# Deformable convolution network on Trainium2: variances from a moving operand, and an earlier first statistic with half of the rows kept

## The chip, the cores and the metric

The kernel runs on one NeuronCore of a Trainium2 chip (trn2). A core has five engines that work side by side, each with its own instruction queue: TensorE (PE in the profile; its weight loads are listed apart as PEld), VectorE (DVE), ScalarE (ACT), GpSimd (POOL) and SyncE (SP), and 16 DMA engines that move data between HBM and the on-chip memories SBUF and PSUM. The metric is the device time of the whole program in microseconds (us), as the median of several runs.

## The reference

The input is x, 8 images of 64 channels, 128x128 pixels, float32. Four layers follow one another, each of the form x = x + layer(groupnorm(x)):

```python
x = x + _L0_conv_ref(_gn(x), ...)   # deformable 3x3 convolution
x = x + _L1_conv_ref(_gn(x), ...)   # 3x3 convolution
x = x + _L2_conv_ref(_gn(x), ...)   # two state-space (S5) blocks, along rows and along columns
x = x + _L3_conv_ref(_gn(x), ...)   # nearest neighbours in a window, and upsampling
```

`_gn` is a group norm over pairs of channels, so every layer needs sums over all pixels of an image before its first output. Layer 0 computes, for every pixel and each of nine taps, an offset (a 1x15 plus a 15x1 convolution, `wh` and `wv`) and a mask (a 3x3 convolution, `wm`), samples the normed image bilinearly at the shifted point, and applies the 64x64x3x3 weights `wd`. It then has a batch norm over all images. Layer 2 begins with a layer norm over the 64 channels of a pixel, `(x - mu) * rsqrt(var + 1e-5) * g + b`; its result feeds a linear recurrence along the pixels, forward and backward.

## The kernel before

**Layout.** Two images make a pair: 64 channels of each fill the 128 partitions, and the 16,384 pixels lie along the free dimension. There are four pairs. Pixels are handled in chunks of 512, 32 a pair. Each engine's instruction order is fixed when the program is built, by a scheduler that follows the order of the program text, the free buffers of each pool, and the data that is ready. A pool tag with one buffer (`bufs=1`) makes the next writer wait for the last reader of that tag.

**Start, pair 0.** `deform` first prepares constants: it issues the zero rows and columns of the four gather tables on ACT's queue (L203 and the two lines after), loads the offset weights and biases on SP's queue (L211 to L232), and copies the weights into `wt` on DVE and POOL (28 of these copies are DVE's, L218). Then:

- `statistics` (L262) loads x in eight pieces of 128x2048 (L267, tag "xs", two buffers), takes `bn_stats` of each quarter (L269), and `groupnorm` turns these into the scale and shift of the norm.
- `fill` (L274) loads x again in eight pieces (L287), norms each on ACT (L288), transposes it on PE (L291), copies it from PSUM into `q`, and writes it pixel by pixel into the gather table in HBM.
- `offsets` (L305) loads a strip `xe` of up to 22 rows (L311), norms it on ACT (L312), runs the offset convolutions on PE with the weights `wt` (L323), evicts on ACT into `ob` (L333), transposes, and computes indices and bilinear weights on DVE (with a sigmoid on ACT, L379).

**Gather stage.** `sample` then issues 9216 indirect DMAs on POOL (L405), each of which fetches four corners of 128 pixels; DVE weights and adds them (L414, L415), PE transposes and multiplies by `wd`. Between them `work` advances two lists of other work by small steps: `near`, the offsets of the next strip, and `far`, the setup of the later layers' constants (`setup_scan` and others, for pair 0), then statistics and fill of the next pair.

**After the gathers**, for each pair: `finish_deform`, `conv3x3` (with the previous pair's nearest-neighbour layer beside it), and `scan_layer`. The latter runs `first_norm` together with the backward scan of the first direction, then the forward scan, then the second direction.

**First norm.** It goes through eight groups (n = 7 to 0) of four chunks. For each chunk PE multiplies by a centring matrix (L887, PSUM tag "x", two buffers), ACT writes the square into `sq` (L889, tags "sq" and "xt" in turn, one buffer each) and the centred values into `bf` (L890), and `variances` (L847) sums the squares over channels on PE:

```python
for q in range(4):
    at = first + 2 * q
    self.nc.tensor.matmul(pv[:, at : at + 2], lhsT=sq[:, q * P : (q + 1) * P], rhs=self.imgmean, start=True, stop=True)
```

Here a quarter of the squares is the stationary operand and the 128x2 matrix `imgmean` (1/64 for the channels of one image) the moving one; the result has pixels on partitions. After four chunks `rsqrt` (L105) computes 1/sqrt(var + eps) on DVE, beginning with the addition of eps (L109). One group later `scale` widens these roots on POOL (`spread`, L857), transposes them back on PE (L860, tag "y", two banks), and multiplies the centred values on DVE (L879). After each group the backward scan makes two steps: `inputs` on ACT (L1205) and four DMAs that rearrange, `drive` (PE L1216 and L1219, a copy to `v` on ACT L1218, two multiplications on DVE, an addition on POOL L1223), and `scan` (PE L1231, ACT L1236, DVE L1238).

Of the kernel before, what the change touches and what calls it, by code (L numbers as in the profile page):

```python
# [9 lines left out]
F32 = mybir.dt.float32  # L10
# [6 lines left out]
P = 128  # L17
C = 64
# [23 lines left out]
class Net:  # L42
# [33 lines left out]
    def setup_constants(self):  # L76
        nc, const = self.nc, self.const
        with self.tc.tile_pool(name="setup", bufs=1) as sp:
# [21 lines left out]
            self.imgmean = const.tile([P, 2], F32, name="imgmean")  # L100
            nc.vector.tensor_copy(self.imgmean, mean.rearrange("p (a b) -> p a b", b=C)[:, :, 0])
# [3 lines left out]
    def rsqrt(self, pool, v, n, eps, tag):  # L105
# [3 lines left out]
        nc.vector.tensor_scalar_add(ve, v, eps)  # L109
# [67 lines left out]
    def deform(self):  # L177
# [6 lines left out]
        with ExitStack() as ctx:  # L184
# [11 lines left out]
            with tc.tile_pool(name="a_setup", bufs=1) as sp:  # L196
                zeros = sp.tile([P, 2 * PW], F32, name="zeros")
                nc.gpsimd.memset(zeros, 0.0)
                for table in (t for pair in tables for t in pair):
                    flat = table.rearrange("a b q -> a (b q)")  # L200
                    n = LINE * PW // P
                    for row in (0, CELL - 1):
                        nc.scalar.dma_start(flat[row : row + 1, :].rearrange("a (p n) -> (a p) n", p=P), zeros[:, 0:n])  # L203
                    for r0, r1 in ((1, CELL - 1 - 1), (CELL - 2, CELL - 1)):
                        nc.scalar.dma_start(flat[r0:r1, 0 : 2 * PW], zeros[0 : r1 - r0, :])
                        nc.scalar.dma_start(flat[r0:r1, (LINE - 2) * PW :], zeros[0 : r1 - r0, :])
                whv = sp.tile([P, 2, 15, 2, 9], F32, name="whv")
                wmm = sp.tile([P, 9, 9], F32, name="wmm")
                for i in range(2):
                    rows = slice(i * C, (i + 1) * C)  # L210
                    nc.sync.dma_start(whv[rows, 0], ins["wh"])  # L211
                    nc.sync.dma_start(whv[rows, 1], ins["wv"])
                    nc.sync.dma_start(wmm[rows], ins["wm"])
                for i in range(2):
                    rows = slice(i * C, (i + 1) * C)
                    for d in range(-7, 8):
                        if d:
                            nc.vector.tensor_copy(wt[rows, at[0, d], 0:2, i, :], whv[rows, 0, d + 7])  # L218
                            nc.gpsimd.tensor_copy(wt[rows, at[d, 0], 0:2, i, :], whv[rows, 1, d + 7])
                    nc.vector.tensor_add(wt[rows, 0, 0:2, i, :], whv[rows, 0, 7], whv[rows, 1, 7])  # L220
                    for a in range(3):
                        for b in range(3):
                            nc.vector.tensor_copy(wt[rows, at[a - 1, b - 1], 2, i, :], wmm[rows, 3 * a + b])
                bh = sp.tile([36, 2], F32, name="bh")
                for d in range(2):
                    for i in range(2):
                        to = slice(18 * d + 9 * i, 18 * d + 9 * i + 9)
                        for n, b in enumerate(("bh", "bv")):
                            nc.sync.dma_start(bh[to, n : n + 1], ins[b][d].rearrange("(k o) -> k o", o=1))
                nc.vector.tensor_add(bias[0:36, :], bh[:, 0:1], bh[:, 1:2])  # L230
                for i in range(2):
                    nc.sync.dma_start(bias[36 + 9 * i : 45 + 9 * i, :], ins["bm"].rearrange("(k o) -> k o", o=1))  # L232
# [205 lines left out]

            run(statistics(0))
            run(fill(0))
            run(offsets(0, 0))
            for p in range(self.npair):
# [951 lines left out]
```

## Time and profile before

| | |
|---|---|
| median of three runs | 18,816.72 us (18,789.93 to 18,832.63) |
| profiled execution, own time | 16,596.21 us |
| profiled span, first to last instruction | 16,594.3 us |
| granted TensorE clock over the span | 0.831 |
| 0 to 167.2 us: constants, statistics, fill, first offsets | 167.2 us, clock 0.97 |
| 167.2 to 11,811 us: gather stage | 11,643.8 us, clock 0.80 |
| first-norm stage, each of four | 183 us, clock 0.77 to 0.78 |
| between the first-norm stages | 974 to 977 us, clock 0.95 |

The profile is one execution recorded by the hardware; its own time stands beside the span of its instructions. Busy times are sums per engine. The granted clock is the TensorE clock that the throttle allowed, as a share of full speed. A line of the timeline gives the start, the duration, the engine, the line of the kernel, the operation with its output and input tiles, and in brackets the idle time ahead of it with the instruction or transfer that ended it. "SPq" marks the issue of a DMA by SP. Durations of a group "xN" cover N instructions in a row.

### The profile page before, as it was taken

The page shows a single profiled execution, that of the slowest core. Times are in us where ns is not written, and L with a number is a line of the kernel's source. Part 1 is how long each engine was busy: PE and PEld are TensorE (multiplying, and loading weights), DVE is VectorE, ACT ScalarE, POOL GpSimd, SP SyncE. Part 2 cuts the span into 40 slices and gives each one's busy share as a digit, 9 for nine tenths or more (in the row PEclk, how much of TensorE's full clock was granted, in tenths as well). Part 3 has the DMA queues.
Part 4 walks back from the last instruction along what each step waited for, and adds up shares of the span by engine and source line. Part 5 has one row for each costly group of instructions (what it writes and reads, how often), then busy time and mean ns, then how long its engine had stood idle before and what let it go on. Part 6 is the DMA issues. An engine that isn't in the chain of part 4 may idle for free. (4 is left out here: it accounts for less than half of the span.)

```text
span 16594.3 us, 119574 instructions
## 1 busy us (share of the span) xinstructions
PE 11150.0 (67%) x31864; PEld 4099.0 (25%) x31864; DVE 11621.1 (70%) x27208; ACT 3000.5 (18%) x5596; POOL 10321.0 (62%) x10484
## 2 busy tenths in 40 slices
PE   6765565756676555657656666563589888988896
PEld 1211111111111111111111111111244444444443
DVE  6777777777777777777777777777557557566666
ACT  1111111111110111111011011000144243343342
POOL 4777777777777777777777777777434134043142
PEclk9987787877798877878887788785689899999897
DMA  5334444444433344443333333333322433334223
GB/s 172 121 116 129 134 136 135 136 130 138 136 119 113 114 130 132 139 131 120 112 115 118 114 115 118 115 111 107 116 71 72 143 79 108 107 80 134 84 68 104
DMA packets 900630, 1937.60 MB, mean 117 GB/s; under 512 B 199916, under 2 KB 435828, under 8 KB 876404
## 3 DMA queue, kind: packets, MB, share of 16 engines
q0 software_dynamic: 442368, 1208.55, 24.6%
q1 hardware_dynamic: 383204, 684.00, 13.5%
q10 hardware_dynamic: 74384, 37.40, 1.1%
q8 instruction: 259, 4.24, 0.1%
q14 instruction: 415, 3.40, 0.1%
HBM read 1544.92 MB, written 208.10 MB: 106 GB/s over the span
## 5 line engine op out<-in xcount | busy, mean ns | idle before, releaser
L405 POOL DMA_INDIRECT g<-table,idx x9216 | 8834.7, 959 | 2809.4 <-issue 2635.5
L414 DVE TENSOR_TENSOR g<-g,wts 128x256 f32<-128x256 f32 x9216 | 3830.9, 420 | 3000.2 <-DMA g<-table,idx 2967.7
L415 DVE TENSOR_REDUCE sm<-g 128x64 f32<-128x256 f32 x9216 | 5014.0, 579 | 0.5
L323 PE MATMUL po<-xe,wt 128*54 128x512 f32 (+3 forms) x8384 | 4576.1, 656 | 34.3 <-ACT ob L333 32.2
L421 PE MATMUL sp<-ident,sm 128*128 128x128 f32 x4096 | 1508.6, 373 | 4021.4 <-DVE sm L415 4011.8
L421 PEld LDWEIGHTS sp<-ident,sm 128*128 128x128 f32 x4096 | 622.3, 154 | 6785.5 <-DVE sm L415 4893.3
L424 ACT COPY s<-sp 128x512 f32<-128x512 f32 x1024 | 599.9, 586 | 7902.6 <-PE sp L421 7902.2
L323 PEld LDWEIGHTS po<-xe,wt 128*54 128x54 f32 x8384 | 902.8, 136 | 1321.4 <-issue 975.8
L429 PE MATMUL yp<-s,wd 128*64 128x512 f32 (+1 forms) x2560 | 906.6, 718 | 30.0 <-ACT s L424 29.8
L857 POOL COPY l_yb<-ln_y 128x512 f32<-128x512 f32 x128 | 79.1, 658 | 1289.2 <-PE l1v L851 1155.3
L1223 POOL TENSOR_TENSOR u<-u,v 128x512 f32<-128x512 f32 x256 | 330.6, 1292 | 700.2 <-DVE v L1222 519.5
L580 PE MATMUL c<-room,l_w 128*64 128x508 f32 (+1 forms) x3072 | 742.1, 597 | 21.6 <-DMA room<-nx 15.5
L1315 POOL TENSOR_TENSOR ms<-ms,ln_y 128x512 f32<-128x512 f32 x256 | 278.3, 1107 | 742.5 <-DVE ln_y L119 710.4
L1205 ACT ACTIVATE fx<-room,ln_b,ln_g 128x512 f32<-128x512 f32 x512 | 639.5, 1294 | 123.8 <-DMA in<-fx 105.7
L423 PE MATMUL s<-ident,sm 128*64 128x128 f32 x1024 | 344.4, 336 | 433.1 <-DVE sm L415 397.2
L1238 DVE TENSOR_TENSOR_SCAN z<-tabs,z,u 128x256 f32<-128x256 f32 x512 | 445.0, 902 | 207.4 <-POOL u L1223 194.0
L1216 PE MATMUL pv<-in,tabs 128*128 128x512 f32 x1024 | 537.6, 649 | 45.4 <-DVE u L1222 45.4
L1285 PE MATMUL py<-in,outs 128*128 128x512 f32 x1024 | 505.8, 607 | 3.7 <-ACT h L1287 2.3
L1302 PE MATMUL pc<-outs,h 128*128 128x256 f32 x2048 | 501.2, 395 | 10.0 <-DVE h L1288 8.8
L1285 PE MATMUL py<-x,outs 128*128 128x512 f32 x1024 | 501.8, 594 | 5.9 <-POOL x L1270 5.3
L1270 POOL TENSOR_TENSOR x<-x,xt 128x512 f32<-128x512 f32 x256 | 350.5, 1369 | 126.1 <-DVE xt L1269 125.8
L1302 PEld LDWEIGHTS pc<-outs,h 128*128 128x128 f32 x2048 | 384.4, 196 | 170.1 <-issue 64.8
(406 smaller groups left out, 10029.6 us busy)
## 6 DMA issues: line engine op xcount, KB each, us to landing
g<-table,idx POOLq DMA_INDIRECT x9216, 2.7
in<-fx SPq DMA_DIRECT2D x1024, 128.0 KB
xe<-in_x_dram SPq DMA_DIRECT2D x56, 1408.0 KB
table<-q SPq DMA_DIRECT2D x256, 256.0 KB
xs<-in_x_dram SPq DMA_DIRECT2D x32, 1024.0 KB
xt<-in_x_dram SPq DMA_DIRECT2D x32, 1024.0 KB
y<-ys SPq DMA_DIRECT2D x128, 256.0 KB
room<-in_x_dram SPq DMA_DIRECT2D x64, 512.0 KB
```

The lines of the kernel that those rows point to most:

```text
L323: nc.tensor.matmul(po[:, r0:r1, c0:c1], lhsT=wt[:, t, :], rhs=xe[:, row + r0 : row + r1, c0 + dx : c1 + dx], start=n == 0, stop=n == len(u ...
L405: nc.gpsimd.indirect_dma_start(out=tq[:, k, :], out_offset=None, in_=flat[i], in_offset=bass.IndirectOffsetOnAxis(ap=idx[:, at : at + 1], ...
L414: nc.vector.tensor_mul(t[:, k], t[:, k], w)
L415: nc.vector.tensor_reduce(sm[:, k], t[:, k].rearrange("p q c -> p c q"), axis=mybir.AxisListType.X, op=ALU.add)
L421: nc.tensor.transpose(sp[:, j, :], sm[:, j * P : (j + 1) * P], self.ident)
L424: nc.scalar.copy(st[i][:, 0:4, m * P : (m + 1) * P], sp)
L429: nc.tensor.matmul(yp[i * C : (i + 1) * C, :], lhsT=wd[0:rows, j, :], rhs=st[i][0:rows, j, :], start=j == 0, stop=j == 4)
L580: nc.tensor.matmul(o, lhsT=lt, rhs=mv, start=k < 2, stop=k >= len(calls) - 2)
L1205: nc.scalar.activation(fx[:, e].rearrange("p h (o m) -> p h o m", m=self.INNER), src[:, e::2], AF.Identity, bias=w["ln1_b"], scale=w["ln1_g"])
L1216: nc.tensor.matmul(pv, lhsT=tabs[:, at : at + P], rhs=fx[:, :, h, :], start=h == 0, stop=h == 1)
L1285: nc.tensor.matmul(py, lhsT=lt, rhs=mv, start=n == 0, stop=n == len(calls) - 1)
L1302: nc.tensor.matmul(pc[:, i], lhsT=hs[:, h, i, m * P : (m + 1) * P], rhs=self.outs[:, CEN : MIX + P], start=True, stop=True)
```

## The change

Two parts of the kernel change.

**Variances.** `imgmean` becomes 128 x (2 x 16): the mean column of each image, 16 times. For each chunk `variances` now makes one product with `imgmean` as the stationary operand and the 512 squares as the moving one; it fills 32 partitions of one PSUM bank, and the four chunks of a group lie below one another in the 128 partitions. After the four, ACT copies the bank to SBUF (`vs`, which takes the single buffer of tag "sq"), `by_pixel` transposes it in four pieces into a bank of tag "y", and `rsqrt` reads one of each 16 equal columns. The text puts the copy ahead of `scale` of the group before, and the transposes and the root behind it. [...]

**Start.** The statistics of pair 0 come first in the program. The last four of their eight pieces go into buffers of their own (`kept`, pool `a_first`, 4 x 2048 columns), and `fill` norms and transposes these in place of loading them again; the first four pieces are loaded twice as before. The preparation of weights, biases and table borders comes after the statistics in the text, with its DMAs on ACT's queue in place of SP's and 28 copies on ACT in place of DVE. The `wd` loads stay on SP's queue, behind the statistics. The pools `a_first` and `a_setup` end before the gather stage; the constants of the later layers take that space.

```diff
-            self.imgmean = const.tile([P, 2], F32, name="imgmean")
-            nc.vector.tensor_copy(self.imgmean, mean.rearrange("p (a b) -> p a b", b=C)[:, :, 0])
+            self.imgmean = const.tile([P, 2, 16], F32, name="imgmean")
+            nc.vector.tensor_copy(self.imgmean, mean.rearrange("p (a b) -> p a b", b=C)[:, :, 0:16])
...
-        nc.vector.tensor_scalar_add(ve, v, eps)
+
+        to = ve if len(v.shape) == 2 else ve.rearrange("p (a b c) -> p a b c", b=v.shape[2], c=v.shape[3])
+        nc.vector.tensor_scalar_add(to, v, eps)
...
-            with tc.tile_pool(name="a_setup", bufs=1) as sp:
-                zeros = sp.tile([P, 2 * PW], F32, name="zeros")
-                nc.gpsimd.memset(zeros, 0.0)
-                for table in (t for pair in tables for t in pair):
...
-            def statistics(p):
+            def statistics(p, kept=()):
+
+
 
                 st = wp.tile([P, NCH, 6], F32, tag="gst", name=f"st{p}")
                 for n in range(8):
-                    xs = xp.tile([P, 2048], F32, tag="xs", name=f"xs{p}_{n}")
+                    xs = kept[n] if n in kept else xp.tile([P, 2048], F32, tag="xs", name=f"xs{p}_{n}")
...
-                            xs = xp.tile([P, 16, H], F32, tag="xs", name=f"xt{p}_{g}")
-                            xf = xs.rearrange("p h w -> p (h w)")
-                            nc.sync.dma_start(xf, self.x[p * P : (p + 1) * P, g * CH : (g + 4) * CH])
+                            held = g // 4 in kept
+                            xf = kept[g // 4] if held else xp.tile([P, 2048], F32, tag="xs", name=f"xt{p}_{g}")
+                            xs = xf.rearrange("p (h w) -> p h w", w=H)
+                            if not held:
+                                nc.sync.dma_start(xf, self.x[p * P : (p + 1) * P, g * CH : (g + 4) * CH])
                             nc.scalar.activation(xf, xf, AF.Identity, bias=nb, scale=r)
...
-            run(statistics(0))
-            run(fill(0))
+            with tc.tile_pool(name="a_first", bufs=1) as fp:
+                kept = {n: fp.tile([P, 2048], F32, name=f"kept{n}") for n in range(4, 8)}
+                run(statistics(0, kept))
+                with tc.tile_pool(name="a_setup", bufs=1) as sp:
+                    whv = sp.tile([P, 2, 15, 2, 9], F32, name="whv")
+                    wmm = sp.tile([P, 9, 9], F32, name="wmm")
+                    for i in range(2):
+                        rows = slice(i * C, (i + 1) * C)
+                        nc.scalar.dma_start(whv[rows, 0], ins["wh"])
+                        nc.scalar.dma_start(whv[rows, 1], ins["wv"])
+                        nc.scalar.dma_start(wmm[rows], ins["wm"])
...
+                        for d in range(-7, 8):
+                            if d:
+                                nc.scalar.copy(wt[rows, at[0, d], 0:2, i, :], whv[rows, 0, d + 7])
+                                nc.gpsimd.tensor_copy(wt[rows, at[d, 0], 0:2, i, :], whv[rows, 1, d + 7])
...
+                                nc.scalar.dma_start(bh[to, n : n + 1], ins[b][d].rearrange("(k o) -> k o", o=1))
+                    nc.vector.tensor_add(bias[0:36, :], bh[:, 0:1], bh[:, 1:2])
...
+                    zeros = sp.tile([P, 2 * PW], F32, name="zeros")
+                    nc.gpsimd.memset(zeros, 0.0)
+                    for table in (t for pair in tables for t in pair):
+                        flat = table.rearrange("a b q -> a (b q)")
+                        n = LINE * PW // P
+                        for row in (0, CELL - 1):
+                            nc.scalar.dma_start(flat[row : row + 1, :].rearrange("a (p n) -> (a p) n", p=P), zeros[:, 0:n])
...
+                wt = wt.rearrange("p t d i k -> p t (d i k)")
+                nc.sync.dma_start(wd[:, 0:4, :], ins["wd"][0:512].rearrange("(j p) o -> p j o", p=P))
+                nc.sync.dma_start(wd[0:C, 4, :], ins["wd"][512:576])
+                run(fill(0, kept))
...
-    def variances(self, pv, first, sq):
-
+    def variances(self, pv, m, sq):
+
+
+        self.nc.tensor.matmul(pv[32 * m : 32 * m + 32, :], lhsT=self.imgmean.rearrange("p a b -> p (a b)"), rhs=sq, start=True, stop=True)
+
+    def by_pixel(self, vs, tag):
+
+        nc = self.nc
+        tq = self.ps.tile([P, 4, P], F32, tag="y", name=f"{tag}_vt")
         for q in range(4):
-            at = first + 2 * q
-            self.nc.tensor.matmul(pv[:, at : at + 2], lhsT=sq[:, q * P : (q + 1) * P], rhs=self.imgmean, start=True, stop=True)
+            nc.tensor.transpose(tq[:, q, :], vs[:, q * P : (q + 1) * P], self.ident)
+        return self.rsqrt(self.small, tq.rearrange("p q (m i r) -> p m q i r", i=2, r=16)[:, :, :, :, 0], 32, EPS, "ln32")
...
-            pv = self.ps1.tile([P, 32], F32, tag="small", name=f"l1v{p}_{n}")
+            pv = self.ps1.tile([P, CH], F32, tag="small", name=f"l1v{p}_{n}")
...
-                self.variances(pv, 8 * m, sq)
+                self.variances(pv, m, sq)
+            vs = wp.tile([P, CH], F32, tag="sq", name=f"vs{p}_{n}", bufs=1)
+            nc.scalar.copy(vs, pv)
             if late:
                 scale(*late)
-                yield
-            late = n, self.rsqrt(self.small, pv, 32, EPS, "ln32")
+            y = self.by_pixel(vs, f"l1_{p}_{n}")
+            if late:
+                yield
+            late = n, y
```

## The prediction

> **What bounds the kernel now.** I read the page first, then the busy time by stage, then the first 170 us and one of the four first-norm stages in order of time.
>
> ```profile
> L405 POOL DMA_INDIRECT g<-table,idx x9216 | 8834.7, 959 | 2809.4 <-issue 2635.5
> ...
> L857 POOL COPY l_yb<-ln_y 128x512 f32<-128x512 f32 x128 | 79.1, 658 | 1289.2 <-PE l1v L851 1155.3
> ```
>
> The gathers run from 167.2 to 11,811 us, 1.26 us apart, and nearly all idle time between them is the engine's own issue. So this stage is as long as POOL's 9216 gathers, and work before it is worth what it shifts the first gather. The second row's wait is POOL with nothing to do during the 3x3 convolutions; it costs nothing.
>
> ```profile
> 0.00:72.00 72.00, 1.17 (x4) 1.00 (x4) 51.09 (x276) 1.69 (x3) 11.71 (x53) 1.00 0.60 211
> 72.00:167.20 95.20, 81.89 (x268) 31.81 (x269) 39.14 (x108) 41.65 (x47) 0.41 (x2) 0.95 0.89 261
> 167.20:11820.00 11652.80, 7087.45 (x16883) 1951.77 (x16883) 8623.16 (x20310) 1251.01 (x2545) 8836.95 (x9225) 0.80 0.41 123
> ...
> 12063.00:12246.00 183.00, 152.82 (x577) 94.23 (x576) 88.70 (x214) 92.89 (x131) 39.86 (x48) 0.78 0.28 71
> ```
>
> Columns: window, length, busy PE, weight loads, DVE, ACT, POOL (instructions), granted clock, DMA share, GB/s. The last row is the first-norm stage of pair 0 (first square to the forward scan's first output); the others also last 183 us, 733 in all. PE is the busiest engine there, at a clock of 0.78, where the stages around it have 0.95. Two stretches therefore matter: the start, and these four.
>
> ```profile
> 28.73 0.91 SPq L267 DMA_DIRECT2D xs<-in_x_dram  x2
> ...
> 72.03 4.08 ACT L288 ACTIVATE xt<-xt,gn_nb,gn_y 128x2048 f32<-128x2048 f32 x2 [30.48 <-DVE gn_nb L147]
> ...
> 156.89 2.73 ACT L312 ACTIVATE xe<-xe,gn_nb,gn_y 128x2816 f32<-128x2816 f32 x1 [3.56 <-DMA xe<-in_x_dram]
> ...
> 161.07 0.68 ACT L333 ACTIVATE ob<-po,bias 54x512 f32<-54x512 f32 x1 [1.09 <-PE to L336]
> ```
>
> At the start the statistics' first load is issued only at 28.7, behind weights, biases and scan constants; the norm is known at 72.0; then PE (82 of 95 us) and the DMA engines (share 0.89) are both nearly full. PE ends the second offset convolution at 149.9, but its eviction comes at 161.1, since ACT waits in order for the next strip. The first gather follows at 167.2.
>
> ```profile
> 12064.40 0.95 PE L851 MATMUL l1v<-imgmean,sq 128*128 128x2 f32 x8
> ...
> 12082.04 4.88 ACT L1205 ACTIVATE fx<-room,ln_b,ln_g 128x512 f32<-128x512 f32 x4
> ...
> 12087.56 1.51 PE L887 MATMUL pc<-room,center_r 128*128 128x512 f32 x2 [2.60 <-ACT room L890]
> 12088.87 1.70 PE L851 MATMUL l1v<-imgmean,sq 128*128 128x2 f32 x8
> ```
> ```profile
> 12070.00:12080.00 10.00, 10.00 (x68) 7.84 (x67) 5.66 (x22) 6.19 (x10) 2.27 (x4) 1.00 0.00 0
> 12080.00:12090.00 10.00, 6.91 (x32) 4.43 (x32) 3.83 (x15) 8.10 (x10) 2.29 (x4) 0.91 0.38 83
> 12090.00:12100.00 10.00, 10.00 (x35) 6.90 (x36) 4.49 (x17) 4.59 (x6) 0.00 (x0) 0.58 0.11 24
> ```
>
> In each group of four chunks ACT's four scan inputs (L1205, 4.9 us) stand ahead of the next squares; PE idles some 2.6 us and the clock falls to half for about 10 us: the same eight variance pieces take 0.95 us before and 1.70 after.
>
> [...]
>
> **Variances, part by part.** Removed per chunk: four matmuls whose stationary side is a quarter of the squares, [...]. Added per chunk: one matmul with a 128x32 stationary side and 512 moving columns, two pieces. The offset convolution is the nearest row (54 columns, 512 moving: 0.43 to 0.5 us a piece), so 0.86 to 1.0. PE neither gains nor loses by itself. Added per group: a copy of the bank to SBUF on ACT (the 128x512 copy L1218: 0.59), four transposes [...], and the wait chain copy, transposes, reciprocal root. The copy takes the buffer of the squares (tag "sq", one buffer), so square 0 of the next group waits for the transposes; behind it in ACT's queue wait the identities, the scan inputs and the scan's copies. The transposes share the two "y" banks with the spread scales and stand behind them on PE.
>
> By the instruction order of the changed kernel a steady group holds pc 3.4, variances 3.4, scales 1.7 [...], drive 2 x (1.72 + 0.86), scan steps 0.6, transposes 0.4: 14.7 us of PE at full clock, before 14.3. The gap: ACT's v copy, the last scale multiply, two inputs 2.5, z, two inputs 2.5, z, square 0.7 make 8 us from the last drive to the first variance, in which PE has 4 us of work: 4 idle, as before (12163.6 to 12167.1). So 18.7 at full clock, 18.3 before. Before, the last three groups take 23.0 on average (variance ends 12134.1, 12158.8, 12179.3, 12203.2), so half clock costs it 4.7. In the new order what follows the gap is almost all 512-column streaming. The trace's record of the clock has half-clock spells of 10.2 to 13.7 us in the first-norm stages (three to four steps of 3.41 us), but in the gather stage, where PE streams with pauses, 169 of some 310 spells last one step. I assume one such short spell per group, half of 3.4 us lost: 1.7, so 20.4, or -2.6 a group, four groups: -10. Bounds: none, -4.3 each; a spell as long as now or a little longer, up to +2.5.
>
> The head loses: in groups 7 to 4 the root of a group comes later by copy, transposes and the shared buffer (1 us), and group 5's first square stands behind all four inputs: idle from 12082.8 to 12089.2 by the chain, 6.4 against 2.8 now; the second block is fully exposed too. Sum +5 to +10, I take 6. The tail, 43 us from the last variance to the forward scan, gets the copy and transposes: +1. Together -3 a pair, -12 for four; bounds -9 and +25 a pair (-36 and +100).
>
> **The start, part by part.** Weights, biases and border zeros go from SP to ACT's queue; scan constants, whose space now lies under the kept rows, move behind the table writes on SP; 28 wt copies move from DVE to ACT (some 0.2 each, 6 us while ACT is idle). The first load is issued at 0.75. A pair of loads lands 5.6 us after issue (28.73 to 34.31). With two rotating and four own buffers the eight loads need about 28 us at the 300 GB/s of the fill, but each waits for an earlier transfer on its own semaphore lane: the last kept load for a border zero, which ACT issues after the 28 copies and the third rotating load. By that chain: last load issued 26, landed 32, statistics (2.46) 34.5, aggregate to norm 7.0 (65.05 to 72.03): 41.5 instead of 72.0, or 30 earlier. ACT must then do two strips, four kept blocks and several copies before the offset strip (about 18 us, against 6 before), which costs PE's convolution some 14 us; transposes fill part. PE then has 25 transposed groups x 0.6 and 54 us of convolution: ends near 132. In exchange the eviction is no longer behind the next strip (11 us), and four reads, 4.2 MB or 14 us of DMA at 300 GB/s, are gone. From eviction to first gather 6.1 as now: 138.5, or -28. Bounds: lanes and ACT late, -10; nothing late, -35. DVE's scan constants (about 30 us) move under the gathers, where DVE has 26% free and four gather buffers: nothing; without that cover 30.
>
> **Sum.** -12 - 28 = -40 against the profiled execution's own 16,596.21 (span 16,594.3). The timed median, 18,816.72, is 2220 higher; the page doesn't show where, so I carry the difference over: 18,777.
>
> **Rivals.**
> The clock stays full: steady groups 18.7, A = -36, in all -64, 18,753. For it: long streams; against: a 4 us gap remains. Chance 0.20.
> The clock doesn't recover, so the chain lengthens every group: spells of three to four windows as now, 23.5 to 25.5 a group. Then +8 to +25 a pair, middle +20, four pairs +80, less 28: +52, 18,869, slower. It decides from a steady group of 23.6 us on (no gain in the variances). For it: fuller ACT (+0.6 a group) and the serial copy-transpose chain; against: less weight loading. Chance 0.25.
> The start's gain doesn't come: ACT's zero writes, in order ahead of the first strip, hold the fill as SP's queue does now. -12 - 5 = -17, 18,800. For it: 24 such writes took ACT 18.7 us before (7.57 to 26.25). Against: they can end near 30. Chance 0.10.
> That the change doesn't do what it says is excluded for the instructions, which the order shows; the rest is timing.
>
> **Numbers.** The likeliest (0.45): 18,777, own range 18,745 to 18,805. The runs before span 43 us; 0.2% is 38 us, about what a measurement of this kernel can tell. The range reaches from the full clock with half the runs' spread below it, 18,730, to the slow-clock case and a little over, 18,880. Faster (below 18,779): 0.6 of the likeliest, nearly all of the first rival: 0.46. Slower (above 18,854): three quarters of the second rival: 0.19. The rest 0.35.
>
> **What would show it.** Right: first gather near 138, norm near 41; first-norm stages near 180 with a clock above 0.85; half-clock spells of one or two windows; the gather stage as long as now. Wrong: stages above 190 with the same clock; an eviction of the offsets still behind a load; POOL waiting for DVE in the first hundreds of gathers.

## The result and the profile after

The changed kernel takes 18,725.29 us (median of 20 runs, 18,673.71 to 18,776.63), the kernel before 18,795.13 us (20 runs, 18,723.15 to 18,851.25). The ratio is 0.9966, with a 95% interval of 0.9955 to 0.9978: 64 us faster (41 to 85). The forecast was 40 us. The median of 18,725 lies just below the low end of the stated range, 18,730; but the kernel before, too, came out 22 us lower over 20 runs than over the three that the prediction started from. In what follows a gain in us is taken from the ratio, unless two medians stand beside it.

One thing has to be said on the totals first. The profiled execution of before, on which the sums were made, took 16,596 us; that of the changed kernel took 18,752. The two differ in the gather stage, 11,642 against 13,840 us from first to last indirect DMA. It is no effect of the change, since the kernel before has both lengths too: on three chips used below it takes 16,615 to 16,631 us, on the fourth 18,776. (There is no profile of it at the longer time; that its extra time lies in the gather stage, too, is taken from the changed kernel's profiles.) So stages are compared, not spans.

The busy time of the changed kernel by stage (window, its length, busy time of PE, weight loads, DVE, ACT and POOL with their instructions, granted clock, DMA share, GB/s): start up to the norm, norm to first gather, gather stage, and the first-norm stages of pairs 0 and 1.

```profile
0.00:45.47 45.47, 1.17 (x4) 1.00 (x4) 27.20 (x86) 4.46 (x29) 10.14 (x45) 1.00 0.84 291
45.47:139.00 93.53, 83.35 (x275) 32.81 (x276) 39.87 (x131) 38.13 (x46) 1.63 (x11) 1.00 0.81 240
139.00:13980.00 13841.00, 7154.88 (x16858) 1973.79 (x16856) 8430.68 (x20443) 1247.21 (x2548) 9526.12 (x9225) 0.71 0.34 104
14235.50:14416.20 180.70, 146.55 (x417) 57.79 (x417) 81.61 (x214) 97.75 (x139) 38.05 (x48) 0.84 0.28 72
15392.20:15569.70 177.50, 143.53 (x416) 56.85 (x416) 81.62 (x214) 97.64 (x139) 37.95 (x48) 0.85 0.28 73
```

The norm is known at 45.5 instead of 72.0. The stretch from there to the first gather is hardly shorter, 93.5 against 95.2 us, with the same PE work of 82 to 83. In the first-norm stage weight loads fall from 94 to 57 us, PE's busy time from 153 to between 144 and 147, and the clock rises from 0.78 to between 0.84 and 0.85; ACT is busy 5 us longer.

The changed kernel's start in order of time:

```profile
0.74 5.64 SPq L231 DMA_DIRECT2D xs<-in_x_dram  x2
...
45.47 4.08 ACT L254 ACTIVATE xt<-xt,gn_nb,gn_y 128x2048 f32<-128x2048 f32 x2 [29.06 <-DVE gn_nb L149]
...
61.65 2.73 ACT L278 ACTIVATE xe<-xe,gn_nb,gn_y 128x2816 f32<-128x2816 f32 x1
...
131.74 0.68 ACT L299 ACTIVATE ob<-po,bias 54x512 f32<-54x512 f32 x1 [12.67 <-PE po L289]
...
139.00 1.18 POOL L371 DMA_INDIRECT g<-table,idx  x1 [17.50 <-DVE up L348]
```

The first load is issued at 0.74 and the offsets' eviction is now released by PE itself, 12.7 us after ACT had run out of work, not by a strip of x. The first gather comes at 139.0, 28.2 us earlier.

A steady group of the first-norm stage, first in windows of 10 us, then its main instructions:

```profile
14340.00:14350.00 10.00, 7.31 (x12) 1.60 (x11) 4.70 (x16) 6.57 (x11) 3.08 (x5) 0.66 0.60 157
14350.00:14360.00 10.00, 10.00 (x42) 5.17 (x41) 5.30 (x11) 4.53 (x7) 1.28 (x1) 1.00 0.00 0
```
```profile
14337.06 0.60 PE L865 MATMUL l_vt<-ident,vs 128*128 128x128 f32 x4
...
14337.98 2.54 ACT L1224 ACTIVATE fx<-room,ln_b,ln_g 128x512 f32<-128x512 f32 x2 [0.52 <-DVE room L894]
...
14340.47 2.49 ACT L1224 ACTIVATE fx<-room,ln_b,ln_g 128x512 f32<-128x512 f32 x2
...
14342.89 0.68 ACT L904 ACTIVATE sq<-pc,cns 128x512 f32<-128x512 f32 x1
...
14343.63 1.91 PE L858 MATMUL l1v<-sq,imgmean 128*32 128x512 f32 x2 [1.03 <-ACT sq L904]
...
14352.20 1.05 PE L858 MATMUL l1v<-sq,imgmean 128*32 128x512 f32 x4
```

The first line is the transposes of the variances of the group before. The four scan inputs still stand ahead of the squares, and PE still idles behind them. What has changed is what follows: the variance product at 14,343.6 runs at half clock (1.91 us for two pieces), but 9 us later the clock is full. By the trace's record of the clock a half-clock spell lasts 6.8 us here, two steps of 3.41, where it lasted 10.2 to 13.7. The groups follow each other at 20.5 us, against 23.0.

The variances themselves take about as much of PE's time as before, though now at a higher clock, as the costliest PE groups of a stage show, first of before, then of the changed kernel in its profile on another chip (pieces | busy us, mean ns of one | idle before):

```profile
L851 PE MATMUL l1v<-imgmean,sq 128*128 128x2 f32 x256 | 39.5, 278 | 8.5 <-ACT sq L889 8.1 <-ACT z L1236 0.5
```
```profile
L902 PE MATMUL pc<-room,center_r 128*128 128x512 f32 x62 | 39.5, 736 | 0.0
...
L858 PE MATMUL l1v<-sq,imgmean 128*32 128x512 f32 x64 | 35.1, 765 | 9.0 <-ACT sq L904 9.0
...
L865 PE MATMUL l_vt<-ident,vs 128*128 128x128 f32 x32 | 4.8, 273 | 0.0
```

39.5 us of quarter products have become 35.1 us of streaming and 4.8 us of transposes. The 6 to 9 us that PE's busy time lost come from the other rows, which run at a higher clock: the drive (L1216, in the changed kernel L1235) took 773 ns a piece, and takes 657.

The same steady group also occurs at other clocks. In the first stage of the kernel with the new variances alone, the last four groups are, from the end of one group's variance products to the end of the next group's:

```profile
12107.23:12126.65 19.42, 16.72 (x55) 6.82 (x54) 10.02 (x27) 11.61 (x17) 4.82 (x6) 0.91 0.31 81
12126.65:12144.30 17.65, 14.96 (x53) 6.50 (x53) 10.03 (x27) 11.61 (x17) 4.83 (x6) 1.00 0.34 90
12144.30:12163.60 19.30, 16.60 (x55) 6.79 (x53) 10.02 (x27) 11.62 (x17) 4.82 (x6) 0.91 0.31 83
12163.60:12184.20 20.60, 17.90 (x55) 7.05 (x53) 10.02 (x27) 11.61 (x17) 4.82 (x6) 0.83 0.29 76
```

PE's idle time is 2.7 us in each. With no half-clock spell a group takes 17.7 us, with a spell of one step 19.3 to 19.4, with two steps 20.5 to 20.6. So here one step costs 1.7 us and two cost 2.8 to 2.9.

### The profile page after: what moved, and what is told of

Read it like the earlier page. It is cut to its first block, busy times and chain, and to the rows that moved or that the text cites. A ratio compares the mean times of both kernels' runs of the same rounds, so it can differ in the third digit from the quotient of the medians.

```text
span 18750.6 us, 118297 instructions
## 1 busy us (share of the span) xinstructions
PE 11197.3 (60%) x31224; PEld 3936.2 (21%) x31224; DVE 11380.1 (61%) x27180; ACT 3014.3 (16%) x5658; POOL 11001.5 (59%) x10484
## 5 line engine op out<-in xcount | busy, mean ns | idle before, releaser
L371 POOL DMA_INDIRECT g<-table,idx x9216 | 9524.1, 1033 | 4332.4 <-issue 2626.4
L381 DVE TENSOR_REDUCE sm<-g 128x64 f32<-128x256 f32 x9216 | 5064.9, 580 | 3480.1 <-remote 2659.1
L289 PE MATMUL po<-xe,wt 128*54 128x512 f32 (+3 forms) x8384 | 4712.7, 672 | 832.1 <-ACT ob L299 572.1
L380 DVE TENSOR_TENSOR g<-g,wts 128x256 f32<-128x256 f32 x9216 | 3557.6, 415 | 529.5 <-DMA g<-table,idx 464.9
L396 DVE BATCH_NORM_STATS2 ystat<-yp 128x6 f32<-128x512 f32 x128 | 89.3, 697 | 818.5 <-PE yp L395 372.8
L395 PEld LDWEIGHTS yp<-s,wd 128*64 128x64 f32 (+1 forms) x2560 | 225.3, 159 | 1500.1 <-ACT s L390 797.6
L1235 PE MATMUL pv<-in,tabs 128*128 128x512 f32 x1024 | 508.9, 619 | 46.7 <-DVE u L1241 45.5
```

Of the source, the lines that this page charges most:

```text
L289: nc.tensor.matmul(po[:, r0:r1, c0:c1], lhsT=wt[:, t, :], rhs=xe[:, row + r0 : row + r1, c0 + dx : c1 + dx], start=n == 0, stop=n == len(u ...
L371: nc.gpsimd.indirect_dma_start(out=tq[:, k, :], out_offset=None, in_=flat[i], in_offset=bass.IndirectOffsetOnAxis(ap=idx[:, at : at + 1], ...
L380: nc.vector.tensor_mul(t[:, k], t[:, k], w)
L381: nc.vector.tensor_reduce(sm[:, k], t[:, k].rearrange("p q c -> p c q"), axis=mybir.AxisListType.X, op=ALU.add)
L395: nc.tensor.matmul(yp[i * C : (i + 1) * C, :], lhsT=wd[0:rows, j, :], rhs=st[i][0:rows, j, :], start=j == 0, stop=j == 4)
L1235: nc.tensor.matmul(pv, lhsT=tabs[:, at : at + P], rhs=fx[:, :, h, :], start=h == 0, stop=h == 1)
```

## The experiments

All with five rounds against the kernel before on the same chip. First the two parts singly, beside a repetition of the kernel before.

**The kernel before against itself.**

> The kernel before, unchanged, timed against itself: it measures what five rounds can tell. Both theories: ratio 1.000 within 0.0015. Its profile answers where the 2220 us between the first profiled execution (16,596 us) and the median of the runs lie: theory, all in the gather stage (first to last indirect DMA 13,840 us as in the changed kernel's profile, against 11,642), with the first gather again at 167 and first-norm stages of 183 us. Rival: spread over all stages through a lower clock, so first-norm stages above 200 us.

Measured: ratio 1.0001 (0.9993 to 1.0010). First gather at 168.1, gather stage 11,645 us, first-norm stages 183.3, 184.1, 192.0 and 183.8. Five rounds can tell some 0.1%, and a stage of the same program can be 8 us longer in one pair than in the next. This chip has the short gather stage, so it didn't answer the question of the 2220 us; the changed kernel's profile above speaks for the gather stage, and two later variants of it on a fourth chip (gather stages of 13,813 and 13,737) agree.

**Only the variances.**

```diff
+        self.nc.tensor.matmul(pv[32 * m : 32 * m + 32, :], lhsT=self.imgmean..., rhs=sq, start=True, stop=True)
...
+            vs = wp.tile([P, CH], F32, tag="sq", name=f"vs{p}_{n}", bufs=1)
+            nc.scalar.copy(vs, pv)
...
+            y = self.by_pixel(vs, f"l1_{p}_{n}")
```

> Only the variances are changed, the start is that of before. Theory: the four first-norm stages fall by 2.6, 6.6, 5.9 and 5.7 us as in the changed kernel's profile, 21 us in all, ratio 0.9989; first gather at 167, gather stage unchanged. Rival (the parts interact or the rest of the 64 us comes from here): ratio below 0.998.

Measured: 16,578.05 against 16,623.5, ratio 0.9975 (0.9967 to 0.9982), 42 us faster (30 to 55). The stages last 172.1, 177.5, 178.2 and 172.0 us. This is more than the 21 us that comparing one profile with one profile gave. Stages from all profiles explain most of it:

- the old variances, 16 stages in four profiles (before, its repetition, and the two kernels of the start below): 178.8 to 195.5, mean 185.8;
- the new variances, 12 stages in three profiles: 172.0 to 180.7, mean 177.5.

The difference of the means is 8.3 us a stage, 33 us for four pairs, with a wide margin: the four stages of one profile add up to between 726 and 769 us with the old variances and to between 700 and 716 with the new. The long ones have one thing in common. Four of the 16 old stages last 192.0 to 195.5 us, and just in these a half-clock spell that begins some 14 us ahead of the stage goes on for 44.4 us, thirteen steps. In the others, which last 178.8 to 184.1, the spell there takes 6.8 to 13.7 us and is over within 3 us of the stage's start. The profile of before, on which the forecast stood, holds none of the long ones. In the twelve new stages no spell is longer than 17.1 us.

**Only the start.**

```diff
+            with tc.tile_pool(name="a_first", bufs=1) as fp:
+                kept = {n: fp.tile([P, 2048], F32, name=f"kept{n}") for n in range(4, 8)}
+                run(statistics(0, kept))
+                with tc.tile_pool(name="a_setup", bufs=1) as sp:
...
+                run(fill(0, kept))
```

> Only the start is changed, the variances are those of before. Theory: first gather at 139 in place of 167, nothing else moves: 28 us, ratio 0.9985. Rival (the gather stage itself also becomes shorter, for the 15 us that the profile's two parts leave open): ratio 0.9977 or below, and a gather stage that is 15 us shorter than in the other profile of the same kind.

Measured: 16,579.89, ratio 0.9976 (0.9965 to 0.9986), 40 us faster (23 to 58). The first gather comes at 137.5, 30.6 us earlier than in the repetition of before. The gather stage lasts 11,650 us, against 11,645: it isn't shorter, so the rival's extra 15 us aren't there, and the measured time, whose interval reaches down to 23, doesn't ask for them. What this profile has beyond the 30.6 us lies in the unchanged first-norm stages, 726 us for four against 743 in the repetition, none of them a long one.

**The start without kept rows.**

```diff
-                kept = {n: fp.tile([P, 2048], F32, name=f"kept{n}") for n in range(4, 8)}
+                kept = {}
```

> As the start-only kernel, but no row is kept: all eight pieces of x go through the two rotating buffers and are loaded again for the fill. It tells the order of the work at the start from the kept rows. Theory: the norm is known later than 45 us, since each load waits for the statistics of the one two before (8 pieces of about 5 us each: some 45 to 50 us), and the fill loads 4.2 MB more, 14 us of DMA at 300 GB/s; first gather at 150 to 158, ratio 0.9993. Rival (the kept rows do nothing, PE's transposes and convolutions set the time): first gather at 139 to 143, ratio 0.9986.

Measured: 16,609.74, ratio 0.9993 (0.9985 to 1.0001). From its timeline:

```profile
57.36 4.08 ACT L252 ACTIVATE xt<-xt,gn_nb,gn_y 128x2048 f32<-128x2048 f32 x2 [40.88 <-DVE gn_nb L147]
...
132.04 2.09 ACT L252 ACTIVATE xt<-xt,gn_nb,gn_y 128x2048 f32<-128x2048 f32 x1 [1.09 <-DMA xt<-in_x_dram]
146.13 0.68 ACT L297 ACTIVATE ob<-po,bias 54x512 f32<-54x512 f32 x1 [1.12 <-PE to L300]
...
152.24 1.18 POOL L369 DMA_INDIRECT g<-table,idx  x1 [2.87 <-DVE up L346]
```

The norm comes at 57.4, 7 us later than the expected 45 to 50, and the last piece of x for the fill waits for its transfer until 132.0. The first gather, at 152.2, is 15 us later than with kept rows. So of the start's 30 us about half is the order of the work and half the kept rows, which here means both the buffers of their own and the reads that they save.

**The changed kernel on another chip.**

> The changed kernel itself, on the chip on which the two parts were timed singly (0.9975 and 0.9976). Theory (the parts don't meet: one shifts the first gather, the other shortens four stages 12 ms later): the two add up, ratio 0.9951. Rival (they share something, so that one gain covers part of the other): 0.9966 or above, as on the chip of the first comparison.

Measured: 16,549.67 against 16,614.66, ratio 0.9961 (0.9948 to 0.9975), 65 us, much as in the first comparison. The run fell on another chip than the single parts did, contrary to what was expected. The two single gains add to 82 us; the interval here, 42 to 86 us, holds both theories' values, so times alone don't separate them. In the profile the first gather comes at 137.4, as with the start alone. The stages, of 180.5, 177.7, 177.5 and 180.3 us, are 16 us longer in sum than with the variances alone (716 against 700), which is about what is missing to 82. Their code is the same; they differ in the number of half-clock steps (the clock of the first stage is 0.84 here and 0.88 there). So neither gain is seen to cover part of the other, but that the two simply add is not shown.

**Streaming added to the old variances.** The result of the added product is read by nobody. (The bank `pv` and the matrix `imgmean` are widened for it as in the changed kernel.)

```diff
+        self.nc.tensor.matmul(pv[0:32, 32:CH], lhsT=self.imgmean..., rhs=sq[:, 32:CH], start=True, stop=True)
```

> The kernel before with work added: after the four quarter products of each chunk PE also multiplies the same squares as a moving operand by the 128x32 mean matrix, 480 columns, into unused columns of the same bank, and nobody reads it. 128 x 2 pieces of some 0.4 us, 26 us of PE per first-norm stage at full clock, more at half. Theory A (512-column streams end a half-clock spell, weight loads don't): spells fall from three or four steps of 3.41 us to one or two and the stage clock rises from 0.78 to 0.83 or more; the added work is mostly paid back, stages of 188 to 200 us instead of 183 to 195, ratio 0.9995 to 1.0030. Theory B (a spell's length is set by the idle gap ahead of it, whatever PE does then): spells and clock as before, stages of 215 us and more, ratio 1.006 or more.

Measured: 16,681.97, ratio 1.0041 (1.0027 to 1.0054). Its first stage, and the row of the added product in it:

```profile
12077.80:12277.10 199.30, 171.18 (x640) 89.11 (x640) 87.56 (x214) 92.64 (x131) 42.03 (x48) 0.90 0.25 65
```
```profile
L852 PE MATMUL l1v<-sq,imgmean 128*32 128x480 f32 x64 | 33.6, 609 | 0.0
```

The clock rises from 0.78 to between 0.88 and 0.90 and most half-clock spells shrink to one or two steps, although nothing was removed: with streaming after the gap the spell ends sooner. The added work also moves the idle time in a steady group, from gaps of 0.7 to 4.3 us to two of 1.7 and 1.1. That this ends the spells instead is unlikely: the old group with the smallest gaps, two of 0.7 us, has the longest spell of the steady ones, 13.7 us, and the changed kernel's groups, with the same gaps of 1.7 and 1.0, have spells of two steps where these have one. The 33.6 us of added work lengthen the stage by 13 to 18 us (199 to 204 against a mean of 185.8). Theory A has the mechanism, with a payback of about half, not most; the ratio lies between the two theories' ranges.

**Own buffer for the copied variances.** The buffer is one that only the later scan uses.

```diff
-            vs = wp.tile([P, CH], F32, tag="sq", name=f"vs{p}_{n}", bufs=1)
+            vs = wp.tile([P, CH], F32, tag="zb", name=f"vs{p}_{n}", bufs=1)
```

> The changed kernel with one edit: the copied variances have a buffer that nothing else uses in this stage, in place of the buffer of every second square. Theory (the shared buffer costs only the head of the stage, since in a steady group the squares stand behind the scan inputs anyway): stages 2 to 4 us shorter than the changed kernel's 172 to 181, steady groups 20.5 as now, ratio to the changed kernel 0.9993 to 1. Rival (the shared buffer holds each group): steady groups 18.5, stages 14 us shorter, ratio to the changed kernel 0.9966.

Measured: 16,481.99, ratio to before 0.9922 (0.9909 to 0.9936), and so about 0.996 to the changed kernel on the same chip. Its four first-norm stages:

```profile
12040.50:12202.70 162.20, 137.17 (x417) 56.32 (x416) 86.49 (x214) 97.47 (x139) 39.83 (x48) 0.91 0.31 80
13174.70:13339.40 164.70, 139.71 (x416) 57.02 (x416) 86.47 (x214) 97.43 (x139) 39.88 (x48) 0.89 0.30 79
14313.20:14476.10 162.90, 136.32 (x417) 55.98 (x416) 87.39 (x216) 97.56 (x139) 40.50 (x48) 0.92 0.31 81
15449.60:15612.70 163.10, 136.65 (x417) 56.02 (x416) 87.23 (x216) 97.42 (x139) 40.48 (x48) 0.92 0.31 81
```

The rival wins clearly: 163.2 us a stage against 179.0 for the changed kernel, 63 us for four, nearly the whole of the measured difference (16,549.67 to 16,481.99, 68 us). PE's idle time falls from 34 to about 26 us, its busy time from 145 to about 137 by the clock. The shared buffer was not a matter of the head alone: of the 15.8 us, 6 come from the first four groups and 2.7 from each of the last four, which take 16.9, 17.5, 16.8 and 20.0 us in place of 20.5 (the tail gives 1 back); only the last of them still has a half-clock spell, of one step.

Is it a wait for the buffer? In the steady groups of the changed kernel ACT is not seen to wait for it. In the group shown above the transposes, which free the buffer, end at 14,337.7; the next square starts at 14,342.9, right behind the scan inputs and `z` in ACT's order, without a pause. Only ahead of the first squares of the second and third group does ACT idle, for 0.5 and 1.3 us, where with the own buffer it doesn't. What the edit changes is the order fixed at the build: the first squares of the fourth and fifth group now stand ahead of the scan inputs, and the later groups, too, are put together differently. So that the edit is worth 15.8 us a stage is shown; that it works by the order more than by waits is a reading of the trace, since no run holds the order fixed.

**Scaling in the middle of a group.**

```diff
                 self.variances(pv, m, sq)
+                if m == 1 and late:
+                    scale(*late)
+                    yield
...
-            if late:
-                scale(*late)
             y = self.by_pixel(vs, f"l1_{p}_{n}")
             if late:
                 yield
             late = n, y
         scale(*late)
         yield
+        yield
...
             for _ in self.first_norm(wp, p, a, b, r, nb):
                 next(back)
-                next(back)
```

> The changed kernel with the scaling of the group before placed after the second chunk of a group, and one step of the backward scan after the second and one after the fourth chunk, in place of two steps at the end. So ACT's four scan inputs no longer stand in one row ahead of the squares. Theory (the gap of some 3 us behind the four inputs starts each half-clock spell): the gap goes, spells become rare, steady groups 16.5 to 18.5 in place of 20.5, stages 150 to 168, ratio to the changed kernel 0.9965 to 0.9985. Rival (the chain drive, turn, addition, scan through ACT's queue, now behind squares, becomes the bound): steady groups 20.5 or longer, ratio to the changed kernel 1 or more.

Measured: 16,517.08, ratio to before 0.9944 (0.9931 to 0.9958). Steady groups 19.9 us, stages 173.0 to 174.3, clock 0.89 to 0.90. The inputs are split and most spells last one step, as the theory has it, but a group is only 0.6 us shorter and the stages stay above the theory's 168; the rival's 20.5 us or more didn't come either. A group without any spell takes 18.1 to 18.3 us here, against 17.7 in the order of the changed kernel: a high clock is not yet a short group.

**Transposes ahead of the scaling, buffer shared.**

```diff
+            y = self.by_pixel(vs, f"l1_{p}_{n}")
             if late:
                 scale(*late)
-            y = self.by_pixel(vs, f"l1_{p}_{n}")
-            if late:
                 yield
```

> The changed kernel with the shared buffer kept, and the four transposes and the root put ahead of the scaling of the group before instead of behind it. It asks why the own buffer was worth 15 us a stage. Theory A (the buffer is held too long: the squares of the next group wait for transposes that stand behind sixteen spread transposes and both drives on PE, and so fall behind the scan inputs in ACT's order): freed early, the squares stand ahead of the inputs again; steady groups 16 to 19, stages 162 to 170, ratio to before 0.992 to 0.994. Theory B (any sharing costs it, because the copy itself waits for the square before it and the next square for the copy): stages 175 and more, ratio to before 0.996.

Measured: 16,544.02 against 16,631.15, ratio 0.9950 (0.9937 to 0.9964). Its first stage:

```profile
12043.50:12220.00 176.50, 141.94 (x417) 57.08 (x417) 89.21 (x215) 98.06 (x139) 42.69 (x48) 0.90 0.29 74
```

By its time theory B: 176.5 us. The squares do move ahead of the inputs, as theory A has it, and the clock is at 0.90, as with the own buffer. But the four inputs now stand between the second and the third square, PE idles 3.5 us in each steady group, and a group takes 20.6 us; PE's idle time in the stage stays at 34.6 us (176.5 less 141.9). So freeing the buffer earlier doesn't bring what the own buffer brings. Since the order changed with it, this doesn't show that every sharing costs it.

**Both together**, the own buffer and the scaling in the middle, with the edits of those two kernels.

> Own buffer for the copied variances and the scaling in the middle of a group together. Theory A (the two remove different waits: one the late squares, the other the row of four inputs): stages 150 to 158, ratio to before 0.989 to 0.991. Theory B (both only move squares ahead of the inputs, so the second adds nothing, and its own order, which took 23 us in the second group, costs): stages 163 to 172, ratio to before 0.992 to 0.994.

Measured: 16,496.05, ratio 0.9921 (0.9907 to 0.9934). Stages of 161.1 to 165.8, clock 0.92 to 0.95: no better than the own buffer alone (162.2 to 164.7). Theory B. These two are the fastest versions that were run, and level (ratios 0.9922 and 0.9921).

**One and two products more per group.** The added products write the same values once more. The edit for one:

```diff
                 self.variances(pv, m, sq)
+                if m == 3:
+                    self.variances(pv, m, sq)
```

> The changed kernel with one product more per group: the variances of the fourth chunk are computed twice, the same values into the same place, 0.86 us of PE at full clock and 1.7 at half, on the path from the squares to the copy. It asks what sets the changed kernel's group of 20.48 to 20.51 us, which is six clock steps of 3.413. Theory A (groups lock to the clock's steps: a later start of the idle gap moves the end of the half-clock spell by whole steps): steady groups stay at 20.5, stages within 2 us of the changed kernel's 177 to 181, ratio to before 0.996. Theory B (the chain of work sets the group and the six steps are chance): groups of 21.4 to 22.2, stages 6 to 12 us longer, ratio to before 0.9975 to 0.999.

> The same with two products more per group, 1.7 us at full clock. Theory A: steady groups of 20.5 still or of 23.9 (seven steps), nothing in between; stages 177 to 181 or 197 to 205. Theory B: groups of 22.2 to 23.5, stages 12 to 21 us longer, ratio to before 0.999 to 1.001.

Measured, on the chip with the long gather stage: 0.9967 (0.9954 to 0.9980) and 0.9975 (0.9963 to 0.9987). The first stage of each:

```profile
14201.70:14381.20 179.50, 146.40 (x433) 58.85 (x433) 81.70 (x214) 97.75 (x139) 37.96 (x48) 0.87 0.28 72
```
```profile
14135.80:14325.80 190.00, 156.54 (x449) 61.09 (x449) 81.72 (x214) 97.81 (x139) 38.08 (x48) 0.87 0.26 68
```

With one product more a steady group takes 20.2 us and once a stage 18.6, with two more 21.0 and once 22.4. Neither theory's numbers came, but the traces say why. PE's idle time is 2.7 us in all these groups, as in the changed kernel, and their lengths go by the number of half-clock steps:

| half-clock steps in the group | none | one | two |
|---|---|---|---|
| changed kernel, variances alone | 17.7 | 19.3 to 19.4 | 20.5 to 20.6 |
| one product more | 18.6 | 20.2 | |
| two products more | | 21.0 | 22.4 |

At the same number of steps each product costs 0.8 to 1.0 us. So the chain of work sets the group, as in theory B, plus the price of its steps; groups aren't tied to whole steps, and that six steps make 20.48 us is chance. The first product is nearly free because with it most groups have one step in place of two: stages of 179.5 to 180.1 against a mean of 177.5, PE busy for 146 to 147 us, about as in the changed kernel, at a clock of 0.87 instead of 0.84. The second finds no step to save and costs its full price and a little more (+9 us a stage, where 8 x 0.86 is 7; 0.86 us is an estimate for two pieces, from the drive's, which start 0.43 us apart at full clock).

## Why the prediction was right, and where it was off

**The start** was right by its steps. PE's last offset convolution was put at 132 and the eviction follows at 131.7; the first gather at 138.5, and it comes at 139.0 (135.7 to 139.1 in eight later profiles with this start). That the eviction no longer stands behind a strip, and that four reads are worth about 14 us, the runs show (15 us). Too early by 4 us was the norm, 41.5 against 45.5: the last load was put at 26 and is issued at 29.8, behind the waits for earlier transfers. It didn't matter, since ACT's strips and blocks ahead of the first offset convolution cost PE less than was counted: 15.9 us from the norm to that convolution, 7.0 of them filled with transposes, so 9 lost where 14 were put. Two errors cancel here. DVE's scan constants under the gathers, put at nothing, cost some 8 us by the means, which is less than single profiles differ by: on the chips with the short gather stage it lasts 11,641 to 11,664 us with the new start (mean of seven 11,652) and 11,631 to 11,657 with the old one (mean of four 11,644). The third rival, a start whose gain doesn't come, is excluded.

**The variances** were right in mechanism and sign, and off in size: -12 forecast, -33 from the stages' means, -42 timed. The sum of the steps, with the prediction's own bounds (the end of the fourth group's variance products, and of the last group's), as means of the four pairs of the changed kernel's first profile and of the profile of before:

- The head, from the first square: 54.1 us instead of 47.8. Forecast +6; it is +6.4.
- The steady groups: 82.1 us for four instead of 92.8. Forecast -10; it is -10.7.
- The tail: 42.3 us instead of 43.1. Forecast +1, for the copy and the transposes; it is -0.9.

So against the profile that it started from, each of the three terms is right within 2 us, and the sum is -5.2 us a pair in place of -3, -21 for four. The rest of the gain isn't in these terms. It lies in the reference: the prediction took 183 us for the old stage, from four stages of one profile, and put it at nothing that other executions have the long ones of 192 us and more. The mean over 16 stages is 186, 9 us more for four than that profile has. The profiles with the new variances differ too, down to 172 us. By the means the start's 28 us and these 33 make 61 of the 64 us measured.

The steady group's 20.4 us, where 20.5 was measured, was right through two errors of opposite sign, and so partly by luck. At full clock the sum had 18.7 us, with 4 us of idle; the group without a spell above takes 17.7, with 2.7 idle. (The old group that the 4 us were likened to has 3.1.) Against that, one short spell was assumed, for 1.7 us, and two steps are the rule, for 2.8.

What the prediction didn't see is what the shared buffer costs. It named 1 us in the head. Its steady group was counted from the built order, and so holds what the sharing does to that order, as if it could not be otherwise. The run with the own buffer shows that it can: 15.8 us a stage less. In what place of the buffer's use this arises is not settled.

Some sums of the prediction don't agree with its own terms. With +6 in the head and +1 in the tail, the variances would gain nothing from a steady group of some 21.3 us on, not 23.6. Its bounds of -9 and +25 us a pair come to about -11 and +21. That PE neither gains nor loses by the exchange of products was an estimate. In the profile of before the weight loads of the old variances start 112 ns apart at full clock and 213 ns apart at half, so eight of them take 0.9 us and 1.7; the sums above, 39.5 us of PE before against 35.1 and 4.8 after, agree with it, though they stand at different clocks.

Of the rivals, the full clock forecast 64 us in all, which is what was measured, and better than the likeliest case's 40. But its mechanism isn't what happened: it asked for steady groups of 18.7 us, and they take 20.5 at a stage clock of 0.84 to 0.85. That clock is also a little below the 0.85 that the prediction named as a sign of being right. The slower rival needed spells as long as before, 10.2 to 13.7 us; in the steady groups they mostly last 6.8. That half-clock spells are shorter with streaming was argued from the gather stage; the run with added streaming shows it, with one or two steps for most spells and a stage clock of 0.88 to 0.90 in place of 0.78.

In the traces the changes of the clock fall on a grid of 3.413 us: in the profile of before all 749 changes, in the changed kernel's all 731, lie within 1 ns of it over the whole span. The phase goes with the spread that misled the reference. Counted in parts of a step from the grid to the start of the stage's first square, the four long old stages begin at 0.88, 0.00, 0.07 and 0.10, all others at 0.35 to 0.77. New ones at 0.03 and 0.06 last 172.1 and 172.0 us, at 0.28 to 0.47 177.5 to 178.2, at 0.57 to 0.63 180.3 to 180.7. This is what 28 stages have in common, no experiment: no run shifted a stage on purpose. Nor does it hold for every order of work. With the scaling in the middle of a group, stages at 0.01, 0.39, 0.55 and 0.86 all last 173.0 to 174.3 us.

## What to carry to other kernels

In these runs PE idled for a few microseconds again and again, and what it did after the gap bore on how long it stayed at half clock: 512-column streams mostly brought it back in one or two steps of 3.4 us, rows of weight loads with two columns in three or four, and at times only in thirteen. A new temporary that borrows a single buffer from a loop can cost time in every turn of it (here 2.7 us in each of a stage's last four groups), even where ACT is not seen to wait for the buffer; most likely because the order of instructions is built around it. Price it by giving it a buffer of its own, if only as a trial. And a stage's length in one profile is one draw; take its mean over all repetitions in all traces at hand before a few microseconds are counted.

## What the runs showed of the hardware

Three things were new to me. The length of one and the same stage differs by up to 17 us in 180 (178.8 to 195.5), and in the 28 stages counted above goes with its phase to the clock's steps. An extra streaming product, worth 0.8 to 1.0 us of a group at the same number of half-clock steps, lengthened the stage by 2 to 3 us only, though it came eight times, since most groups then had one half-clock step fewer.

And the gather stage differs between executions on different chips by 2.1 to 2.2 ms. In the long form POOL's waits between 1000 and 9000 us of the changed kernel's profile are (time, number, longest):

```profile
POOL g L371 <- issue: 1515.7, 4951, 5.6
POOL g L371 <- DVE sm L381: 845.4, 201, 26.4
POOL g L371 <- DVE g L380: 57.7, 50, 18.5
```

In the short form the profile of before has, in the same stretch, 74.6 us for the second row and no wait of any kind above 0.3 us. In the long form ACT stands still for up to 55 us and DVE for up to 42 us at a time, while POOL goes on issuing until it waits for DVE in its turn, up to 26.4 us at a time. What stops them no run here shows.
